# Two attention blocks on one core: the first sum of exponentials, the statistics and the inverted sums are moved

## The chip, the core and the metric

The kernel runs on one core of a Trainium2 chip. The metric is the device time of one launch in microseconds (us), smaller is better. Five engines work side by side, each with its own instruction stream: TensorE (PE; PEld are its weight loads), VectorE (DVE), ScalarE (ACT), GpSimd (POOL) and SyncE (SP), which issues the DMAs here.

## The reference

Eight images of 512 channels and 32 x 32 pixels pass through two layers of the same kind; all is float32.

```python
def layer(x, gn_w, gn_b, wq, bq, wk, bk, wv, bv, wp, bp):   # x: (8, 512, 32, 32)
    xn = group_norm(x, 8 groups, eps=1e-5) * gn_w + gn_b
    q, k, v = (xn @ w.T + b  for w, b in ((wq, bq), (wk, bk), (wv, bv)))   # 1024 tokens, 512 channels
    attn = softmax(q @ k.T * 64 ** -0.5)                    # 8 heads of 64 channels
    return x + (attn @ v) @ wp.T + bp
out = layer(layer(x, layer 0's weights), layer 1's weights)
```

## The kernel before

**Jobs.** A job is one image in one layer: 16 jobs, in the order images 0 and 1 in layer 0, images 0 and 1 in layer 1, images 2 and 3 in layer 0, and so on (`jobs`, L100). The main loop (L941 to L1005) works for step n at the attention of job n and then at the products of job n + 1, while job n + 2's normalisation is being prepared.

**Phases of a step.**
- Attention of job n (`Attention.run`, L724). There are 8 groups, each a pair of heads and a half of the queries, and 8 steps in each group. A step makes scores (`scores`, L641: eight products of 64 x 64 tiles), their exponential on ScalarE (L656), the running sum of the exponentials on VectorE (L660 for the first two, L662 for the rest) and, two steps later, the products with v (`values`, L664). At certain steps a "chore" of the next job is recorded: the statistics of its normalisation (`reads`, steps 4, 8, 12, 16 and 17), its groups' means and its scaling (`steps`, from step 24), and the sums of blocks `t[0]`, `t[1]` (steps 56 and 60).
- The v products of job n + 1 (`v_phase`, L420), the output products of job n (`proj_phase`, L454) and the k and q products of job n + 1 (`deep_phases`, L491).

These products are made by block formulas with seven products instead of eight (`chain`, L377, once for v and output, twice nested for k and q). In a chain the products with numbers 1, 5, 6, 2, 7, 3, 4 are accumulated in four PSUM banks named z, y, u and w. Products 1, 6, 7 and 4 use the same bank, so product 4 waits until the result of product 7 is taken from it (`put`, L540: L549 or L551 on VectorE). In `deep_phases` there are seven chains for k (numbers 0 to 6) and seven for q (7 to 13); two chains are always interleaved, each in its half of the PSUM. After product 7 and after product 3 of a chain one waiting addition of larger blocks (L567, collected in `outer`) is recorded. The last three products of the last q chain are recorded after the first two scores of the attention (L1001 to L1004), so that in this place no other chain stands between products 7 and 4.

**Order.** The orders on TensorE, ScalarE and VectorE are as written in the program; the tile framework adds the waits. `later(delay, fn)` records `fn` when an estimated clock, advanced by hand (`advance`), has gone on by `delay`.

**The end of a group** (`finish`, L681). VectorE reduces the sums over the rows and transposes the result (L688, to `r`). Four DMAs bring `r` to 32 partitions (`lr`, L694). ScalarE copies one half of the values' products from PSUM (L697) and VectorE adds the other half into q's place (L698), which frees the PSUM banks. Some 7.6 us later `invert` (L702) adds the four parts, inverts and transposes them (L706 to L708), sends them to DRAM (`rd`, L709), follows the largest sum and inverse (L710, L711), and two DMAs spread the result over 64 partitions each (`rb`, L713). At 14.6 us `normalise` multiplies (L718). After the last group of a job the delays are 6.0 and 11.5, and `out_sums` (L759) reads the result from 12.6 on.

**Weights.** They come through a ring of eight tiles (`fetch`, L166), each fetched when a tile is released. For the first job of a layer `prepare` (L188) makes the inner weight sums of k and q on VectorE, four operations for each chain. For job 0 the outer weight sums too are made on the way: `factor` (L148) for v0, k0 and q0; q0 stands in the place of image 1's tile.

Of the kernel before, what the change touches and what calls it, by code (L numbers as in the profile page):

```python
# [18 lines left out]
P = 128  # L19
# [51 lines left out]
def fast_path(  # L71
# [20 lines left out]

    out_bias = acts.tile([P, 2, NC], F32, name="out_bias")
    bias_step = acts.tile([P, 2, 2, 2], F32, name="bias_step")
    lmax = acts.tile([RP, RP], F32, name="lmax")
    nc.gpsimd.memset(lmax, 1.0)
    rmax = acts.tile([RP, RP], F32, name="rmax")
    nc.gpsimd.memset(rmax, 1.0)

    jobs = [(b0 + i, layer) for b0 in range(0, B, 2) for layer in range(2) for i in range(2)]  # L100
# [7 lines left out]
    def advance(us):  # L108
        clock[0] += us
        due = [t for t in todo if t[0] <= clock[0]]  # L110
        for t in due:
            todo.remove(t)
            t[1]()
# [101 lines left out]
    class Norm:  # L215


        def __init__(self, n):
            b, layer = jobs[n]
            self.n, self.layer, self.xt = n, layer, xs[b]  # L220
            self.stats = small.tile([P, NC, 2, 6], F32, tag="stats", name=f"stats_{n}")
            self.mv = small.tile([P, NC, 2], F32, tag="mv", name=f"mv_{n}")
            self.mr = small.tile([P, NC, 2], F32, tag="mr", name=f"mr_{n}")
            self.mul = small.tile([P, NC], F32, tag="mul", name=f"mul_{n}", bufs=1)

        def stat(self, cc):
            for sh in range(2):
                nc.vector.bn_stats(
                    self.stats[:, cc, sh, :], self.xt[:, cc, sh * HALF : (sh + 1) * HALF]
                )  # L230
            nc.vector.bn_aggr(
                self.mv[:, cc, :], self.stats[:, cc, :, :].rearrange("p s k -> p (s k)")
            )

        def gather(self):

# [29 lines left out]

        def scale(self, cc, cols=slice(0, S)):
            nc.vector.tensor_scalar(
                xn[0][:, cc, cols], self.xt[:, cc, cols], self.mr[:, cc, 0:1],
                self.mul[:, cc : cc + 1], ALU.subtract, ALU.mult,  # L270
            )

# [29 lines left out]
    def norm_steps(n):  # L302
        norm = Norm(n)

        def scale(cc):
            if cc == 0:
                norm.factors(slice(0, NC))
                xn[0] = acts.tile([P, NC, S], F32, tag="xn", name=f"xn_{n}")
            norm.scale(cc)

        shift = norm.shift
        reads = [lambda cc=cc: norm.stat(cc) for cc in range(NC)] + [norm.gather]
        steps = [norm.groups]
        for cc in range(NC + 1):
            def both(cc=cc):
                if cc > 0:
                    shift(cc - 1)
                if cc < NC:
                    scale(cc)
            steps.append(both)  # L320
        return reads, steps
# [166 lines left out]

        return half_phase(n, O, src, to, group, ORDER)

    def deep_phases(n):  # L491


        layer = jobs[n][1]
        dst = {}
        chains = [(K, o) for o in OUTER] + [(Q, o) for o in OUTER]
# [89 lines left out]
        def thunk(c, j):  # L586
            def go():
                if j == 0:
                    live[c] = begin(c)
                live[c](ORDER[j])  # L590
                if ORDER[j] in (7, 3) and outer:
                    outer.popleft()()
                if j == 6:
                    end(c)
                    if c + 1 == len(chains):
                        while outer:
                            outer.popleft()()
                advance(0.43)

            return go  # L600
# [30 lines left out]
    class Attention:  # L631
# [8 lines left out]

        def scores(self, i):  # L641
            n, q, k = self.n, self.q, self.k
            groups, steps, es, acc = self.groups, self.steps, self.es, self.acc
            g, kc = steps[i]
            hp, sh = groups[g]
            sc = two_banks("sc", f"sc_{n}_{i}")
# [8 lines left out]
            e = epool.tile([P, 2, HALF], F32, tag="e", name=f"e_{n}_{i}")  # L655
            nc.scalar.activation(e, sc, AF.Exp, scale=SCALE)  # L656
            es[i] = e
            if kc == 1:
                acc[g] = apool.tile([P, 2, HALF], F32, tag="acc", name=f"acc_{n}_{g}")
                nc.vector.tensor_add(acc[g], es[i - 1], e)  # L660
            elif kc > 1:
                nc.vector.tensor_add(acc[g], acc[g], e)  # L662

# [15 lines left out]
                    )  # L679

        def finish(self, g):  # L681
            n, q = self.n, self.q
            groups, acc, po = self.groups, self.acc, self.po
            hp, sh = groups[g]
            cols = slice(sh * HALF, (sh + 1) * HALF)
            a = acc.pop(g)
            r = small.tile([P, RP], F32, tag="r", name=f"r_{n}_{g}")
            nc.vector.tensor_reduce(  # L688
                r, a.rearrange("p j (b e) -> p (j b) e", e=RP), AX.X, ALU.add,
                apply_transpose=True,  # L690
            )
            lr = small.tile([RP, NQ, RP], F32, tag="lr", name=f"lr_{n}_{g}")
            for i in range(NQ):
                nc.sync.dma_start(lr[:, i, :], r[i * RP : (i + 1) * RP, :])  # L694
            p = po.pop(g)
            px = apool.tile([P, HALF], F32, tag="px", name=f"px_{n}_{g}")
            nc.scalar.copy(px, p[:, 0, :])  # L697
            nc.vector.tensor_add(q[:, hp, cols], p[:, 1, :], px)  # L698
            rd = dram.tile([2, HALF], F32, tag="rd", name=f"rd_{n}_{g}")
            rb = apool.tile([P, HALF], F32, tag="rb", name=f"rb_{n}_{g}")  # L700

            def invert():  # L702
                lt = small.tile([RP, RP], F32, tag="lt", name=f"lt_{n}_{g}")
                ri = small.tile([RP, RP], F32, tag="ri", name=f"ri_{n}_{g}")
                rt = small.tile([RP, RP], F32, tag="rt", name=f"rt_{n}_{g}")
                nc.vector.tensor_reduce(lt, lr.rearrange("p a b -> p b a"), AX.X, ALU.add)  # L706
                nc.vector.reciprocal(ri, lt)
                nc.vector.transpose(rt, ri)  # L708
                nc.sync.dma_start(rd.rearrange("j (b e) -> (j b) e", e=RP), rt)  # L709
                nc.vector.tensor_max(lmax, lmax, lt)  # L710
                nc.vector.tensor_max(rmax, rmax, ri)  # L711
                for j in range(2):
                    nc.sync.dma_start(  # L713
                        rb[j * HD : (j + 1) * HD, :], rd[j : j + 1, :].to_broadcast([HD, HALF])
                    )

            def normalise():
                nc.vector.tensor_mul(q[:, hp, cols], q[:, hp, cols], rb)  # L718

            ends = g + 1 == len(groups)  # L720
            later(6.0 if ends else 7.6, invert)
            later(11.5 if ends else 14.6, normalise)

        def run(self, chores):  # L724

            steps = self.steps
            for i in range(2, len(steps) + LEAD):
                if i < len(steps):
                    self.scores(i)
                self.values(i - LEAD)  # L730
                g, kc = steps[i - LEAD]
                if kc == NT - 1:
                    self.finish(g)
                    advance(0.85)
                if i in chores:
                    chores[i]()
                advance(1.71)

    def judge():
        nc.vector.tensor_max(lmax, lmax, rmax)  # L740
        worst = small.tile([RP, RP], F32, tag="worst", name="worst")
        nc.vector.tensor_copy(worst, lmax)
        nc.vector.tensor_reduce(worst[:, 0:1], lmax, AX.X, ALU.max)
        turned = small.tile([RP, RP], F32, tag="turned", name="turned")
        nc.vector.transpose(turned, worst)
        top = small.tile([1, 1], F32, tag="top", name="top")
        nc.vector.tensor_reduce(top, turned[0:1, :], AX.X, ALU.max)
# [131 lines left out]
            norm.scale(cc, cols)  # L879
            norm.shift(cc, cols)  # L880

    norm.stat(0)
    norm.stat(1)
    mean, var = norm.means_by_products(0, lambda: idle_products(0, "y", "again_a"))
    mean()
    var()
    for i in range(3):
        idle_products(i % 2, "y", f"again_b{i}")
    norm.stat(2)
    norm.factors(slice(0, 2))  # L890
    normed((0, 1), left)
    normed((0, 1), right_)
    nc.gpsimd.tensor_add(v0[:, S1], v0[:, S3], v0[:, A22])
    norm.stat(3)
    first[0]()
    mean, var = norm.means_by_products(1, lambda: None)
    mean()
# [31 lines left out]

    deep_sums(0, 0.2, 12.0)  # L930
    later(5.0, first_plan)
    for part in range(4):
        later(16.0 + 0.9 * part, lambda part=part: factor(q0, part))
    later(20.0, lambda: store_factors(q0, 0, Q))
    later(21.0, lambda: store_factors(v0, 0, V))
    later(30.0, lambda: load_x(1))
    for thunk in first[6:-1]:
        thunk()
    advance(0.0)
# [1 line left out]
    for n in range(-1, len(jobs)):  # L941
        last = n + 1 == len(jobs)
        if n >= 0:
# [2 lines left out]
                w = plain_weights(n)  # L946
            else:
                t = sums(n + 1)
                chores = dict(zip((4, 8, 12, 16, 17), reads))
                chores.update(zip((24, 36, 40, 44, 48, 52), steps))  # L950
                chores.update({56: t[0], 60: t[1]})
                more = {}
# [29 lines left out]
            for thunk in proj[:-1]:  # L982
                thunk()
            rest = proj[-1:]
        both = deep_phases(n + 1)
        prepare((n + 1, K, OUTER[0]))
        prepare((n + 1, K, OUTER[1]))
        both[0]()
# [1 line left out]
        if n >= 0 and jobs[n][1] == 1 and jobs[n][0] + 2 < B:  # L990
            x_tile(jobs[n][0] + 2)
            load_x(jobs[n][0] + 2)
        reads = steps = []
        if n + 2 < len(jobs):
            reads, steps = norm_steps(n + 2)
        for thunk in both[1:-3]:
            thunk()
        att_n = n + 1
# [256 lines left out]
```

## Time and profile before

| what | value |
|---|---|
| median of three runs | 3313.01 us (3311.23 to 3315.83) |
| profiled execution, its own time | 3314.39 us |
| its span, first to last instruction | 3312.6 us |
| mean granted TensorE clock | 0.995 |
| idle time of VectorE before L660, for ScalarE | 54.7 us in 38 waits |
| idle time of VectorE before L706, for the DMA of lr | 75.7 us in 47 waits |
| idle time of VectorE before L718, for the DMA of rb | 36.9 us in 16 waits |
| L228, one bn_stats of 128 x 512 | 0.68 us, 128 times |
| L231, one bn_aggr | 0.21 us, 64 times |
| L706 to L711, one inversion's five operations | 0.36, 0.34, 0.20, 0.14, 0.17 us, 128 times each |

The profile shows one execution. A line such as `L551 DVE ... p<-vd` is the operation of line 551 on VectorE that writes tile p from tile vd. A wait row names the waiting instruction, an arrow, what ended the wait, and then the total in us, how often and the longest. In a timeline the first number is the start from the span's beginning and the second the duration; in brackets is how long the engine was idle before it, and what ended that. Matmuls are pipelined and their ends are modelled, and a few matmul records are missing.

### The profile page before, as it was taken

What the parts mean: (1) busy time and instruction counts of PE and PEld (TensorE: products, weight loads), DVE (VectorE), ACT (ScalarE), POOL (GpSimd) and SP (SyncE); (2) the same over time, 40 slices, a digit from 0 to 9 for tenths busy, and PEclk for the clock granted to TensorE, in tenths of its full rate; (3) what the DMA queues carried; (4) which work ended last, traced back from release to release, by engine and by line L of the source; (5) the groups of instructions that cost most, each with busy time, mean ns of one, the idle gap of its engine ahead of it and who ended that gap; (6) DMA issues with size and microseconds to landing.
All of it is one profiled execution on the core that took longest, in us unless ns stands there. A gap on an engine that the chain in (4) does not pass through costs nothing.

```text
span 3312.6 us, 56298 instructions
## 1 busy us (share of the span) xinstructions
PE 3257.2 (98%) x22240; PEld 1726.5 (52%) x22240; DVE 2588.3 (78%) x3625; ACT 1729.6 (52%) x2561; POOL 25.2 (1%) x32
## 2 busy tenths in 40 slices
PE   9999999999999999999999999999999999999999
PEld 7356373563735537355473554636556364563643
DVE  8886978879687795877958779596795967869676
ACT  4635636356363664636636365463654636546363
POOL 0000000000000000000000000000000000000000
PEclk9999999999999999999999999999999999999999
DMA  8233151230502204032150221304114031130401
GB/s 297 69 105 99 63 161 61 89 120 22 170 22 72 69 25 120 19 103 89 31 164 18 85 59 38 107 19 137 54 41 154 19 102 39 46 98 21 131 24 44
DMA packets 162399, 265.59 MB, mean 80 GB/s; under 512 B 61144, under 2 KB 72528, under 8 KB 161104
## 3 DMA queue, kind: packets, MB, share of 16 engines
q1 hardware_dynamic: 162128, 261.93, 25.7%
q8 instruction: 176, 2.88, 0.4%
q14 instruction: 95, 0.78, 0.1%
HBM read 214.84 MB, written 44.89 MB: 78 GB/s over the span
## 4 chain that ended last, share of the span: by engine, by line
PE 74%; DVE 17%; issue 4%; DMA 3%; SPq 1%; ACT 1%; DVEq 0%; POOL 0%; ACTq 0%
PE sc L651 17%; PE po L676 16%; DVE acc L662 9%; PE vd L535 8%; PE zd L535 7%; PE z L468 6%; PE z L433 5%; PE yd L535 3%; PE ud L535 3%; DVE acc L660 2%; DMA lr<-r 2%; PE v L468 2%; PE y L468 2%; PE u L468 2%; PE y L433 1%
## 5 line engine op out<-in xcount | busy, mean ns | idle before, releaser
L656 ACT ACTIVATE e<-sc 128x1024 f32<-128x1024 f32 x1024 | 1046.6, 1024 | 596.6 <-PE sc L651 537.8
L651 PE MATMUL sc<-q,k 64*64 64x512 f32 x8192 | 1067.4, 594 | 2.2 <-ACT e L656 2.2
L676 PE MATMUL po<-e,v 64*64 64x512 f32 x8192 | 1061.6, 592 | 0.0
L662 DVE TENSOR_TENSOR acc<-acc,e 128x1024 f32<-128x1024 f32 x768 | 936.1, 1219 | 80.6 <-ACT e L656 31.4
L676 PEld LDWEIGHTS po<-e,v 64*64 64x64 f32 x8192 | 310.9, 134 | 574.9 <-issue 561.7
L651 PEld LDWEIGHTS sc<-q,k 64*64 64x64 f32 x8192 | 307.5, 134 | 570.8 <-issue 547.7
L535 PE MATMUL vd<-deep,w 128*128 128x256 f32 x960 | 271.8, 384 | 31.0 <-DVE p L551 30.3
L535 PE MATMUL zd<-deep,w 128*128 128x256 f32 x832 | 232.4, 379 | 0.5 <-DVE p L551 0.5
L535 PEld LDWEIGHTS vd<-deep,w 128*128 128x128 f32 x960 | 179.7, 190 | 74.3 <-DVE p L551 37.2
L660 DVE TENSOR_TENSOR acc<-e,e 128x1024 f32<-128x1024 f32 x128 | 155.3, 1213 | 54.7 <-ACT e L656 54.7
L535 PEld LDWEIGHTS zd<-deep,w 128*128 128x128 f32 x832 | 157.8, 190 | 29.4 <-issue 6.9
L688 DVE TRANSPOSE_TENSOR_REDUCE r<-acc 128x32 f32<-128x1024 f32 x128 | 158.3, 1237 | 0.5
L384 ACT COPY yd<-vd 128x256 f32<-128x256 f32 x128 | 45.7, 357 | 185.4 <-PE vd L535 178.2
L718 DVE TENSOR_TENSOR q<-q,rb 128x512 f32<-128x512 f32 x128 | 86.0, 672 | 36.9 <-DMA rb<-rd 36.9
L468 PE MATMUL z<-to,w 128*128 128x512 f32 x240 | 110.3, 592 | 0.0
L433 PE MATMUL z<-w,xn 128*128 128x256 f32 x480 | 110.1, 382 | 0.0
L433 PE MATMUL z<-w,t 128*128 128x256 f32 x480 | 108.6, 379 | 0.6 <-DVE v L448 0.6
L468 PE MATMUL z<-q,w 128*128 128x512 f32 x240 | 107.9, 592 | 0.0
L706 DVE TENSOR_REDUCE lt<-lr 32x32 f32<-32x128 f32 x128 | 46.3, 362 | 75.7 <-DMA lr<-r 75.7
L433 PEld LDWEIGHTS z<-w,xn 128*128 128x128 f32 x480 | 90.0, 190 | 23.8 <-issue 12.2
L388 ACT COPY u<-z 128x512 f32<-128x512 f32 x62 | 35.3, 570 | 121.8 <-PE z L468 85.1
L433 PEld LDWEIGHTS z<-w,t 128*128 128x128 f32 x480 | 91.2, 190 | 13.5 <-DVE v L448 1.0
(171 smaller groups left out, 3407.7 us busy)
## 6 DMA issues: line engine op xcount, KB each, us to landing
w<-deep SPq DMA_DIRECT2D x196, 448.0 KB
w<-keep SPq DMA_DIRECT2D x226, 256.0 KB
rb<-rd SPq DMA_DIRECT2D x256, 128.0 KB
out_dram<-x SPq DMA_DIRECT2D x64, 256.0 KB
x<-x_dram SPq DMA_DIRECT2D x28, 512.0 KB
deep<-w SPq DMA_DIRECT2D x28, 448.0 KB
keep<-raw SPq DMA_DIRECT2D x5, 1792.0 KB
lr<-r SPq DMA_DIRECT2D x512, 4.0 KB
```

The lines of the kernel that those rows point to most:

```text
L384: nc.scalar.copy(y, z)
L433: nc.tensor.matmul(ps[:, ti * CH : (ti + 1) * CH], r[:, cc, t0 : t0 + P], w[:, cc, :], start=(start and ti == 0 and cc == 0), stop=(cc == ...
L468: nc.tensor.matmul(ps, w[:, cc, i * P : (i + 1) * P], r[:, cc, :], start=(start and cc == 0), stop=(cc == 1), skip_group_check=True,)
L535: nc.tensor.matmul(ps, lhs[:, FACTOR[i], :], moving[i], start=start, stop=True, skip_group_check=True,)
L651: nc.tensor.matmul(sc[h * HD : (h + 1) * HD, j, :], k[r, hp, k0 : k0 + HD], q[r, hp, sh * HALF : (sh + 1) * HALF], start=True, stop=True,)
L656: nc.scalar.activation(e, sc, AF.Exp, scale=SCALE)
L660: nc.vector.tensor_add(acc[g], es[i - 1], e)
L662: nc.vector.tensor_add(acc[g], acc[g], e)
L676: nc.tensor.matmul(po[g][j * HD : (j + 1) * HD, h, :], v[r, kc, d0 : d0 + HD], e[r, j, :], start=(kc == 0), stop=(kc == NT - 1),)
L688: nc.vector.tensor_reduce(r, a.rearrange("p j (b e) -> p (j b) e", e=RP), AX.X, ALU.add, apply_transpose=True,)
L706: nc.vector.tensor_reduce(lt, lr.rearrange("p a b -> p b a"), AX.X, ALU.add)
L718: nc.vector.tensor_mul(q[:, hp, cols], q[:, hp, cols], rb)
```

## The change

Four things are done.

1. `scores` no longer records the running sum for the first two steps of a job; the first sum (L660) is recorded at the start of `run`, behind the last three q products and the additions of `outer`.
2. The statistics are cut into eight pieces (one bn_stats each, every second with its bn_aggr). From job 2 on, the pieces for job n + 2 and the gathering of the means are recorded among the q products of job n + 1, where `outer` is empty after product 7 or 3 of chain 7 and later, with what is left behind the last product. For job 1 the pieces are chores at steps 2 to 10 of job 0's attention. The q0 factors of job 0 are recorded in the same way, from chain 0 on, and the load of image 1 at 12 us.
3. `finish` makes the sums of two groups, an even and the next odd one, into one tile and inverts them together when the odd one is done: four DMAs to `lr` for two groups, one reduction, one inverse, two transposes, one DMA to `rd`, four to `rb`, and two multiplications, one after the other.
4. The first factor of v0 is made by VectorE, ahead of the statistics of the fourth chunk, and no longer by GpSimd. Some small tiles have one buffer in place of two.

```diff
-        def stat(self, cc):
-            for sh in range(2):
-                nc.vector.bn_stats(
-                    self.stats[:, cc, sh, :], self.xt[:, cc, sh * HALF : (sh + 1) * HALF]
+        def stat(self, cc, sh):
+            nc.vector.bn_stats(
+                self.stats[:, cc, sh, :], xs[self.b][:, cc, sh * HALF : (sh + 1) * HALF]
+            )
+            if sh == 1:
+                nc.vector.bn_aggr(
+                    self.mv[:, cc, :], self.stats[:, cc, :, :].rearrange("p s k -> p (s k)")
                 )
...
-        reads = [lambda cc=cc: norm.stat(cc) for cc in range(NC)] + [norm.gather]
+        reads = [lambda cc=cc, sh=sh: norm.stat(cc, sh) for cc in range(NC) for sh in range(2)]
+        reads.append(norm.gather)
...
-    def deep_phases(n):
+    def deep_phases(n, extra=()):
+        extra = deque(extra)
...
-                if ORDER[j] in (7, 3) and outer:
-                    outer.popleft()()
+                if ORDER[j] in (7, 3):
+                    if outer:
+                        outer.popleft()()
+                    elif extra and extra[0][0] <= c:
+                        extra.popleft()[1]()
                 if j == 6:
                     end(c)
                     if c + 1 == len(chains):
                         while outer:
                             outer.popleft()()
+                        while extra:
+                            extra.popleft()[1]()
...
             es[i] = e
+            if i > 1:
+                self.add(i)
+
+        def add(self, i):
+            g, kc = self.steps[i]
+            acc, e = self.acc, self.es[i]
             if kc == 1:
...
         def finish(self, g):
+            n, q, m = self.n, self.q, g % 2
+            hp, sh = self.groups[g]
+            to_ = q[:, hp, sh * HALF : (sh + 1) * HALF]
+            if m == 0:
+                self.r = small.tile([P, 2, RP], F32, tag="r", name=f"r_{n}_{g}", bufs=1)
+                self.place = []
             nc.vector.tensor_reduce(
-                r, a.rearrange("p j (b e) -> p (j b) e", e=RP), AX.X, ALU.add,
-                apply_transpose=True,
+                self.r[:, m, :], self.acc.pop(g).rearrange("p j (b e) -> p (j b) e", e=RP), AX.X,
+                ALU.add, apply_transpose=True,
             )
...
+            self.place.append(to_)
+            if m == 0:
+                return
+            lr = small.tile([RP, NQ, 2, RP], F32, tag="lr", name=f"lr_{n}_{g}", bufs=1)
+            for i in range(NQ):
+                nc.sync.dma_start(lr[:, i], self.r[i * RP : (i + 1) * RP])
...
-                nc.vector.tensor_reduce(lt, lr.rearrange("p a b -> p b a"), AX.X, ALU.add)
+                nc.vector.tensor_reduce(lt, lr.rearrange("p a g b -> p g b a"), AX.X, ALU.add)
                 nc.vector.reciprocal(ri, lt)
-                nc.vector.transpose(rt, ri)
-                nc.sync.dma_start(rd.rearrange("j (b e) -> (j b) e", e=RP), rt)
+                for i in range(2):
+                    nc.vector.transpose(rt[:, i, :], ri[:, i, :])
+                nc.sync.dma_start(rd.rearrange("m j (b e) -> (j b) m e", e=RP), rt)
...
-                for j in range(2):
-                    nc.sync.dma_start(
-                        rb[j * HD : (j + 1) * HD, :], rd[j : j + 1, :].to_broadcast([HD, HALF])
-                    )
+                for i in range(2):
+                    rb.append(apool.tile([P, HALF], F32, tag="rb", name=f"rb_{n}_{g}_{i}"))
+                    for j in range(2):
+                        nc.sync.dma_start(
+                            rb[i][j * HD : (j + 1) * HD, :],
+                            rd[i, j : j + 1, :].to_broadcast([HD, HALF]),
+                        )
...
-            later(11.5 if ends else 14.6, normalise)
+            later(11.5 if ends else 14.6, lambda: normalise(0))
+            later(12.2 if ends else 16.4, lambda: normalise(1))
...
         def run(self, chores):
             steps = self.steps
+            self.add(1)
...
-    nc.gpsimd.tensor_add(v0[:, S1], v0[:, S3], v0[:, A22])
-    norm.stat(3)
+    factor(v0, 0)
+    for sh in range(2):
+        norm.stat(3, sh)
...
-    for part in range(4):
-        later(16.0 + 0.9 * part, lambda part=part: factor(q0, part))
-    later(20.0, lambda: store_factors(q0, 0, Q))
-    later(30.0, lambda: load_x(1))
...
-                chores = dict(zip((4, 8, 12, 16, 17), reads))
+                chores = dict(zip(range(2, 18), reads)) if n == 0 else {}
...
-        both = deep_phases(n + 1)
+        reads = steps = []
+        if n + 2 < len(jobs):
+            reads, steps = norm_steps(n + 2)
+        if n < 0:
+            extra = [(0, lambda part=part: factor(q0, part)) for part in range(4)]
+            extra.append((1, lambda: store_factors(q0, 0, Q)))
+        else:
+            extra, reads = [(7, fn) for fn in reads], []
+        both = deep_phases(n + 1, extra)
...
+        if n < 0:
+            later(12.0, lambda: load_x(1))
```

## The prediction

> **What bounds the kernel now.** First the page's row of busy times:
>
> ```profile
> PE 3257.2 (98%) x22240; PEld 1726.5 (52%) x22240; DVE 2588.3 (78%) x3625; ACT 1729.6 (52%) x2561; POOL 25.2 (1%) x32
> ```
>
> TensorE sets the end. At most its idle 55 us can go, unless some busy time is slow. So next the waits of TensorE alone (total us, times, longest):
>
> ```profile
> PE vd L535 <- DVE p L551: 30.3, 17, 1.8
> PE v L433 <- DVE q L698: 11.8, 10, 2.6
> PE sc L651 <- ACT e L656: 2.2, 4, 0.9
> PE vd L535 <- DVE p L549: 0.7, 1, 0.7
> ```
>
> The first row is one place, met 16 times (1.79 each), and one wait of 1.64 in job 0. The timeline of job 1 shows it, where the last q chain meets the first scores (start, us, instruction, idle before):
>
> ```profile
> 295.27 0.59 PE L535 MATMUL ud<-t,w 128*128 128x256 f32 x2
> 295.98 1.23 DVE L660 TENSOR_TENSOR acc<-e,e 128x1024 f32<-128x1024 f32 x1 [2.04 <-ACT e L656]
> 297.12 0.48 DVE L551 SCALAR_TENSOR_TENSOR p<-vd,vec_sb,s 128x256 f32<-128x256 f32 x1
> 297.52 1.21 DVE L567 TENSOR_TENSOR q<-q,p 128x1024 f32<-128x1024 f32 x1
> 297.65 0.70 PE L535 MATMUL vd<-deep,w 128*128 128x256 f32 x2 [1.79 <-DVE p L551]
> 298.65 0.48 DVE L551 SCALAR_TENSOR_TENSOR p<-ud,vec_sb,s 128x256 f32<-128x256 f32 x1
> 299.23 1.23 DVE L567 TENSOR_TENSOR q<-p,p 128x1024 f32<-128x1024 f32 x1
> ```
>
> The sum of two exponentials (L660) waits for ScalarE at the head of VectorE's queue. Behind it stands the eviction L551, which frees the bank of the last q product.
>
> Then stretches of 3.41 us around the same place (TensorE, weight loads, VectorE, ScalarE, GpSimd busy, granted clock):
>
> ```profile
> 292.29:295.70 3.41, 3.41 (x23) 1.40 (x22) 1.65 (x3) 2.76 (x5) 0.00 (x0) 1.00 0.27 77
> 295.70:299.11 3.41, 1.62 (x11) 0.66 (x14) 3.13 (x4) 0.72 (x2) 0.00 (x0) 1.00 0.02 5
> 299.11:302.53 3.42, 3.42 (x20) 1.05 (x16) 2.46 (x3) 1.02 (x1) 0.00 (x0) 0.50 0.67 187
> 302.53:305.94 3.41, 3.41 (x36) 1.23 (x32) 1.48 (x2) 2.05 (x2) 0.00 (x0) 1.00 0.85 266
> ```
>
> The stretch after the idle one runs at clock 0.50: 20 matmul records instead of 36, "busy" throughout. So the wait is paid twice. Such a half-clock stretch follows at 206.95, 299.11, 916.93, 1121.73, 2145.73, 2350.53, 2555.33, 2760.13 and 2964.93: eight after this wait and one (206.95) after a wait of 2.58 for L698.
>
> [...] The boundaries are multiples of 3.413 us from 206.95; by them the wait lay wholly inside one window in nine jobs, eight of which were throttled (not the one at 506.69), and where it was cut in two, 1.72 us at most falling in one, none was. [...]
>
> **The change part by part.** In the built program the order on TensorE and ScalarE is unchanged; only VectorE, SyncE and one GpSimd operation move.
>
> 1. First sum behind the last product (16 places). L551's operand is ready when the preceding vd products end (295.43 in the matmul records); VectorE starts 0.02 after a product in other rows. So L551 runs 295.45 to 295.93, and the last product starts at about 295.98 instead of 297.65: 1.67 saved. Next late is the second L551 (ud), again behind an L567 of 1.21, at the same distance as before; values wait for it 0.1, as now. 16 x 1.67 = 26.7 gained.
>
> 2. With no idle of 1.79 left there, the eight half-clock stretches go: each costs half of 3.413, 1.71. 8 x 1.71 = 13.7.
>
> 3. Statistics in pieces. bn_stats is 0.68 (L228), the aggregate 0.21. Jobs 1 to 14 do eight pieces among the q products instead of four pairs at attention steps 4 to 16. The room in the q half, VectorE alone, job 6:
>
> ```profile
> 1310.92 0.42 DVE L549 TENSOR_TENSOR p<-vd,s 128x256 f32<-128x256 f32 x1 [1.67 <-PE vd L535]
> 1311.26 1.22 DVE L567 TENSOR_TENSOR q<-p,p 128x1024 f32<-128x1024 f32 x1
> 1312.39 0.42 DVE L549 TENSOR_TENSOR p<-ud,s 128x256 f32<-128x256 f32 x1
> 1313.94 0.48 DVE L551 SCALAR_TENSOR_TENSOR p<-zd,vec_sb,s 128x256 f32<-128x256 f32 x1 [1.13 <-PE zd L535]
> ```
>
> Each chain leaves about 1.0 to 1.7 idle just where a piece of 0.68 or 0.85 goes. An eviction can also be some 0.74 late before TensorE notices (the 1.64 wait: product at 48.33, so due at 46.69; with the 0.245 wait at 63.95 the due time is 63.71 and the undelayed eviction ends near 62.92). Cost nothing; without that cover, 0.85 a chain. Two pieces fall behind the last product, ahead of the first sum: VectorE starts attention 2 to 3 us behind, makes up 0.5 a step (1.22 of work in 1.72), and five e buffers cover it. Exception: job 2, whose chains also prepare weights (four of 0.28, 1.0 in all); there about 0.2 is left per chain, so lateness builds up: 0.8 lost, bounds 0 and 3. Input x for the first-layer statistics has landed: issued at 672.5, last packet 680.8, first piece after 693. The gather's two DMAs wait on SyncE with nothing urgent behind.
>
> 4. Two groups inverted together. One inversion takes 1.08 from L706 to the next sum (0.36 + 0.34 + 0.20 + 0.14 + 0.17); the pair adds 128 elements to the reduction [...], a second transpose (0.20) and little else: 1.5 for two instead of 2.16. What counts is the end of an attention, where VectorE is behind and L698 holds up the second group of v products (second wait row). The timeline there, job 5:
>
> ```profile
> 1229.83 1.22 DVE L333 TENSOR_TENSOR t<-xn,t 128x1024 f32<-128x1024 f32 x1
> 1230.96 0.35 DVE L706 TENSOR_REDUCE lt<-lr 32x32 f32<-32x128 f32 x1
> ...
> 1232.03 3.86 DVE L662 TENSOR_TENSOR acc<-acc,e 128x1024 f32<-128x1024 f32 x3
> 1235.93 1.25 DVE L688 TRANSPOSE_TENSOR_REDUCE r<-acc 128x32 f32<-128x1024 f32 x1
> 1237.10 0.65 DVE L698 TENSOR_TENSOR q<-po,px 128x512 f32<-128x512 f32 x1
> ```
>
> Group 6's inversion vanishes from here (-1.08), groups 5 and 7 each get a second normalising product (+0.6) and lose an inversion; groups 5 to 7 together give about 1.1. Taking 1.1 off each of the ten waits (2.58, 2.59, 1.53, 0.57, 0.18, 1.14, 1.82, 0.87, 0.21, 0.30) leaves 4.2 of 11.8: 7.6 gained (0 to 11.8). The 2.58 falls to 1.5, so its half-clock stretch goes: 1.7.
>
> Against it: in the v phase VectorE waits for rb already (36.9 us in 16 waits, L718). Now four broadcasts of about 0.54 issue stand behind one rd, and two products follow. I take the second product as ending 1.0 later than today's (bounds 0 and 3), 1.7 later against TensorE, which starts earlier. The evictions L448 behind have 1.5 to 2 of slack, but none in job 2 (TensorE waits 0.55 for L448 at 638.97). So 1.7 in job 2, 0.5 in job 0, 0.8 over the rest: 3.0 lost, bounds 0 and 12. The w fetch that stood between rd and rb now stands behind; its weights are a phase away.
>
> 5. Small parts. factor(v0, 0) moves from GpSimd (1.27) to VectorE ahead of the last statistics: 0.7 on the path at the start (TensorE waits for pm at 15.41). The q0 factors run by slots: two of 0.68 leave the queue ahead of the eviction that TensorE awaits at 48.33, 1.2 gained, 0.2 given back at 63.95. load_x(1) now stands ahead of two q-weight fetches; 2 MB take 7 us and those weights were wanted some 10 us after issue: 0.7 lost, bounds 0 and 3. At the end rb's second pair comes about 1.5 later, just as the second half of the last products needs it: 0.3.
>
> Sum: -26.7 - 13.7 - 7.6 - 1.7 - 1.0 + 0.8 + 3.0 + 0.7 + 0.7 + 0.3 = -45.2. The profiled execution took 3314.39 (span 3312.6), so 3269.2; the median of the runs, 3313.01, is 1.4 below it, so 3268.
>
> **The rivals.**
> - The tail wait is replaced (15%): with two pieces and two L567 ahead, exponential 3 waits for its buffer (the final L567 frees it; I find only 0.2 of room) and TensorE loses 1 us in each job. No half-clock stretch. 3268 + 16 = 3284.
> - The half-clock stretches have another cause than the wait (5%): for it, 506.69; against it, eight of nine. 3268 + 15 = 3283.
> - VectorE at the end of attention gains nothing and the late rb costs 1 us a job more (10%): 3268 + 9 + 14 = 3291.
> - Slower (6%): rb late in the v phase. If the second rb lands 6 us later than today's, L448 holds up the v products in all 15 phases by about 4, long enough to halve the clock in most: 15 x (4 + 1) = 75, 3343. Break-even is 3 us a phase, a landing 5 late. For it: SyncE waits 134.7 us for rd landings (128 times, about 1.05). Against: bytes per phase at this point grow by only 256 KB.
> - The change does not do what it says (2%): a wait still keeps L551 behind the first sum. The built order speaks against it; then 3313.
>
> **How the numbers follow.** The forecast has 62%. Its own bounds: all of L698's wait gone and no loss in the v phase, 3268 - 4 - 3 - 3 = 3258; v phase +9, L698 +8, job 0 and 2 +4 do not all come together: 3280. Range of eight in ten, with the rivals at 3283 to 3291: 3257 to 3293. A measurement can tell about 0.2%, 6.6 us, from no change. Faster 0.92 (62 + 15 + 5 + 10), same 0.02, slower 0.06.
>
> **What would show it.** Waits of TensorE: the row vd behind L551 below 6 us, most single waits below 0.3; v behind L698 near 4; granted clock without 0.50 stretches; L706 64 times at about 0.5. Wrong if a new row of more than 10 us stands there (z behind L448, ScalarE's e behind L567), or if the half-clock stretches stay.

## The result, and the profile after

| | median, us | range | of the kernel before |
|---|---|---|---|
| before | 3313.23 | 3311.23 to 3315.83 | |
| after | 3256.66 | 3255.77 to 3257.97 | 0.9829 (95%: 0.9812 to 0.9846) |

The change takes 56.6 us between the medians and 58.6 between the two profiled executions (3314.39 to 3255.77; spans 3312.6 to 3254.0). The forecast took 45.2. The page's row of busy times after:

```profile
PE 3238.2 (100%) x22240; PEld 1730.1 (53%) x22240; DVE 2569.5 (79%) x3371; ACT 1729.5 (53%) x2561; POOL 14.4 (0%) x31
```

The same 22240 products are busy for 19.0 us less: some 15 of them are, by our estimate from the clock record (nine stretches of 3.413 at 0.50, 1.71 each), the half-clock stretches, in which a product counts as busy for longer (in the prediction's stretches 20 matmul records fill 3.42 us at 0.50, 36 fill 3.41 at 1.00). TensorE's idle time fell from 55.4 to 15.8, the other 39.6 of the 58.6. What is left of it, TensorE's waits after (total, times, longest):

```profile
PE vd L538 <- DVE p L554: 3.9, 17, 0.4
PE zd L538 <- DVE p L552: 2.0, 1, 2.0
PE pm L287 <- DVE mv L231: 1.5, 2, 1.0
PE first_y L862 <- POOL blk L65: 1.5, 1, 1.5
PE zd L538 <- DVE p L554: 0.8, 3, 0.3
PE vd L538 <- DVE p L552: 0.6, 1, 0.6
PE z L434 <- ACT xn L274: 0.6, 1, 0.6
```

The old L551 is now L554: 30.3 us became 3.9. The row "v behind L698" (L710 now; 11.8 us) is not there at all, nor is the scores' row for an exponential (2.2) or the v products' row for L448 (0.6). One row is new: 2.0 for L552, in job 0.

The place of the first sum, again in job 1 (the timeline of all engines after):

```profile
288.22 0.48 DVE L554 SCALAR_TENSOR_TENSOR p<-vd,vec_sb,s 128x256 f32<-128x256 f32 x1 [1.59 <-PE vd L538]
288.62 1.22 DVE L570 TENSOR_TENSOR q<-q,p 128x1024 f32<-128x1024 f32 x1
...
288.76 0.70 PE L538 MATMUL vd<-deep,w 128*128 128x256 f32 x2 [0.21 <-DVE p L554]
...
289.75 0.48 DVE L554 SCALAR_TENSOR_TENSOR p<-ud,vec_sb,s 128x256 f32<-128x256 f32 x1
...
290.15 0.69 DVE L227 BATCH_NORM_STATS2 stats<-x 128x6 f32<-128x512 f32 x1
...
292.72 1.17 DVE L674 TENSOR_TENSOR acc<-e,e 128x1024 f32<-128x1024 f32 x1
```

and two stretches of 3.41 us around it (TensorE, weight loads, VectorE, ScalarE, GpSimd busy, granted clock):

```profile
286.71:290.12 3.41, 3.19 (x22) 1.34 (x18) 1.90 (x3) 2.40 (x3) 0.00 (x0) 1.00 0.17 61
290.12:293.54 3.42, 3.42 (x36) 1.22 (x32) 3.39 (x6) 2.05 (x2) 0.00 (x0) 1.00 0.67 197
```

The eviction now waits for the product alone, the first sum starts 4.5 us behind the eviction (292.72 against 288.22), and the next stretch runs at full clock. No stretch up to the last instruction is below 1.00 (mean granted clock 1.000, for 0.995 before).

The end of an attention, in job 5, which the prediction priced: the first v products before (the reduction that belongs to them, at 1235.93, stands in the prediction), then the timeline of all engines after:

```profile
1232.18 3.72 PE L433 MATMUL z<-w,xn 128*128 128x256 f32 x16
```

```profile
1205.50 3.72 PE L434 MATMUL z<-w,xn 128*128 128x256 f32 x16
...
1206.83 1.25 DVE L703 TRANSPOSE_TENSOR_REDUCE r<-acc 128x32 f32<-128x1024 f32 x1
...
1207.99 0.65 DVE L710 TENSOR_TENSOR q<-po,px 128x512 f32<-128x512 f32 x1
```

The reduction starts 1.33 us after the v products begin; before it was 3.75 (1235.93 against 1232.18). This distance, the lateness of VectorE, is what the rest turns on. Over the 15 phases it was 2.8 to 6.2 before and is 1.2 to 2.7 after. TensorE waits for the bank only where it is above about 3.4 (2.91: no wait; 3.41: the second group of v products 0.01 later than without; 3.75: 0.35 later). Where the lateness may come from is in VectorE's own waits, before and then after:

```profile
DVE lt L706 <- DMA lr<-r: 75.7, 47, 4.1
```

```profile
DVE lt L724 <- DMA lr<-r: 23.3, 24, 3.4
```

VectorE stood 75.7 us before inversions whose input had not come, and sums queue up behind such a wait (in job 8, below, three run back to back for 3.86 us from 1792.89, after the wait and its inversion). Whether this lateness lasts until the attention ends is what the experiments ask. By the inversion's place in its attention 17.3 us fall to the second, 44.3 to the third, 3.3 to the fourth and 10.8 to the last. The third in job 8, in the timeline of before:

```profile
1782.72 0.28 SPq L254 DMA_DIRECT2D dg<-ga  x1
...
1783.86 1.28 SPq L257 DMA_DIRECT2D mr<-dg  x2
...
1785.23 2.46 SPq L694 DMA_DIRECT2D lr<-r  x4
...
1791.81 0.36 DVE L706 TENSOR_REDUCE lt<-lr 32x32 f32<-32x128 f32 x1 [3.40 <-DMA lr<-r]
```

The four `lr` DMAs stand behind the normalisation's `dg` (which waits for GpSimd, 56.1 us in 15 waits over the run) and `mr` (which waits for `dg`, 12.0 in 15), and are issued 1.8 us after `r` is complete (1783.45); VectorE idles 3.40. With pairs this group, the third, has no `lr` of its own, so this meeting does not exist.

### The profile page after: what moved, and what is told of

Its sections match the earlier page's. It is cut to its first block, busy times and chain, and to the rows that moved or that the text cites. A ratio compares the mean times of both kernels' runs of the same rounds, so it can differ in the third digit from the quotient of the medians.

```text
span 3254.0 us, 55636 instructions
## 1 busy us (share of the span) xinstructions
PE 3238.2 (100%) x22240; PEld 1730.1 (53%) x22240; DVE 2569.5 (79%) x3371; ACT 1729.5 (53%) x2561; POOL 14.4 (0%) x31
## 4 chain that ended last, share of the span: by engine, by line
PE 97%; DVE 2%; DMA 0%; issue 0%; ACT 0%; SPq 0%; POOL 0%; DVEq 0%
PE sc L659 27%; PE po L690 27%; PE vd L538 8%; PE zd L538 7%; PE z L434 7%; PE z L469 6%; PE yd L538 3%; PE ud L538 3%; PE u L434 2%; PE v L434 2%; PE y L434 2%; PE y L469 2%; PE u L469 2%; PE v L469 2%; PE pp L628 1%; DVE p L554 0%
## 5 line engine op out<-in xcount | busy, mean ns | idle before, releaser
L447 ACT COPY v<-z 128x512 f32<-128x512 f32 x32 | 18.8, 586 | 146.4 <-PE z L434 136.1
```

## The experiments

Three theories stand in the expectations. A: L698's wait went because the statistics left VectorE's queue in the attention. B: it went because of the paired inversions, by the number of VectorE's operations. C, formed after the first runs: it is not the number, but where `lr` stands on SyncE. Each time stands beside that of the kernel before, measured with it. The expectations count by the steps of the prediction: their part 3, the statistics, is part 2 of the change, and their part 4, the pairs, is part 3.

**The first sum alone: before with part 1.**

```diff
             es[i] = e
+            if i > 1:
+                self.add(i)
+
+        def add(self, i):
...
+            self.add(1)
             for i in range(2, len(steps) + LEAD):
```

> The kernel before with part 1 alone: the first sum behind the last q product. Forecast's mechanism: the wait of 1.79 falls to about 0.2 in 16 places (25 us) and the eight half-clock stretches behind it go (14 us): 3274 us, and TensorE still waits 11.8 us for L698, with one half-clock stretch behind the wait of 2.58. Rival, that the half clock has another cause than the wait: 3288 us, with stretches at 0.50 still there. Rival, that part 1 only shifts the wait to the first values or the exponentials: above 3300 us.

3274.15 (before 3314.97), ratio 0.9875 (0.9859 to 0.9892): 40.8 us, for the 40.4 of steps 1 and 2. The L551 row is 5.1 in 17 (16 times 0.21 and the 1.64); all nine half-clock stretches are gone; `v` behind the addition (L704 here) stays at 12.0, and so do the waits for `lr`:

```profile
PE v L433 <- DVE q L704: 12.0, 8, 2.6
```

```profile
DVE lt L712 <- DMA lr<-r: 76.5, 46, 4.3
```

The ninth stretch was expected to stay and went by luck: the wait of 2.58 for the addition is still there, but a boundary between two windows split it into 1.23 and 1.35.

**The changed kernel with the first sum back in place.**

```diff
-            if i > 1:
-                self.add(i)
+            self.add(i)
...
-            self.add(1)
```

> The changed kernel with part 1 undone: the first sum again in the scores. Forecast's mechanism: 16 waits of about 1.8 us return (25 us), and about half of them are followed by a half-clock stretch (0 to 27 us, by where the windows fall): 3282 to 3309 us. If parts 3 and 4 had taken away that wait by themselves: 3257 us.

3303.83 (before 3314.97), ratio 0.9964 (0.995 to 0.9979): 47 above the changed kernel, within the 3282 to 3309 expected. All 16 waits of 1.79 return (25.2 us more), and twelve half-clock stretches (20.5, at 1.71 each), not eight. One of them, as in the stretches shown before:

```profile
697.89:701.30 3.41, 1.62 (x13) 0.61 (x15) 2.84 (x4) 0.96 (x2) 0.00 (x0) 1.00 0.00 0
701.30:704.71 3.41, 3.41 (x24) 1.07 (x20) 3.38 (x6) 1.07 (x2) 0.00 (x0) 0.51 0.28 77
```

With boundaries at multiples of 3.413 from 701.37, thirteen of the waits lie wholly inside a window, of which twelve are followed by half clock (not the last, which ends at 3158.33), and the three that a boundary splits are not (1.4 at most in one window).

**The wait filled: before, with two idle 128x512 products, which the output does not need, in the gap ahead of the last q product.**

```diff
-        for thunk in both[-3:]:
+        for thunk in both[-3:-1]:
             thunk()
+        for i in range(2):
+            idle_products(1, "y", f"fill_{n}_{i}")
+        both[-1]()
```

> The kernel before with two products of 128 x 512 that nobody reads put on TensorE into each of the 16 waits, between products 3 and 4 of the last q chain; the wait for VectorE is as long as before. If idleness inside a window halves the clock: the eight stretches at 0.50 go and the time falls by 14 us, to 0.996 of before, though not one wait for data is shorter. If the half clock has another cause: the time of before, stretches still there.

3303.67 (before 3317.85), ratio 0.9957 (0.9941 to 0.9974). The place in job 1, in the timeline:

```profile
292.57 2.20 PE L837 MATMUL fill<-blk 128*128 128x512 f32 x4
...
294.00 0.48 DVE L551 SCALAR_TENSOR_TENSOR p<-vd,vec_sb,s 128x256 f32<-128x256 f32 x1
...
294.61 0.62 PE L535 MATMUL vd<-deep,w 128*128 128x256 f32 x2
```

The last product starts no earlier after its eviction, and yet the time is 14.2 us lower; the eight stretches that are gone are worth 8 times 1.71, 13.7. So what the half clock followed here was TensorE's idleness (1.79 us in each place before), not what VectorE does meanwhile. One stretch is left, after a wait of 2.57 for L698 in job 1, which was not filled. The rival "another cause" falls.

**The changed kernel with single inversions (without part 3 of the change).** `finish`, `judge` and the small tiles are those of before.

```diff
+            lr = small.tile([RP, NQ, RP], F32, tag="lr", name=f"lr_{n}_{g}")
+            for i in range(NQ):
+                nc.sync.dma_start(lr[:, i, :], r[i * RP : (i + 1) * RP, :])
...
-            lr = small.tile([RP, NQ, 2, RP], F32, tag="lr", name=f"lr_{n}_{g}", bufs=1)
-            for i in range(NQ):
-                nc.sync.dma_start(lr[:, i], self.r[i * RP : (i + 1) * RP])
```

> The changed kernel with part 4 undone: each group inverted alone, and only the last group's normalising product at the end. Theory A (VectorE's lag is made early in an attention, by the statistics and by inversions that wait for lr while it is late, and is never made good): without the statistics the lag stays small, L698 costs under 1 us in all: 3257 to 3260 us. Theory B (what counts is the work of the inversions near the end, as predicted): L698 costs about 11 us again: 3268 to 3272 us.

3267.48 (before 3314.97), ratio 0.9853 (0.9836 to 0.9869).

```profile
PE v L434 <- DVE q L712: 6.1, 3, 2.6
```

```profile
DVE lt L720 <- DMA lr<-r: 41.8, 34, 3.6
```

A's time is missed by 7 us and more. The median lies 0.5 below B's range, and B's reason fails: the wait halves to 6.1, all in jobs 0 to 2, although every inversion is back. In jobs 3 to 14 A's reason holds: the lateness is 1.7 to 1.9 and TensorE does not wait, though third inversions still wait 18.6 us for `lr` there. Beside the first sum alone, this kernel has the statistics' operations and their DMAs moved together, so it does not tell which of them counts. That led to C.

**The changed kernel with the statistics back in the attention.**

```diff
-                chores = dict(zip(range(2, 18), reads)) if n == 0 else {}
+                chores = {
+                    4 + 4 * c: lambda two=reads[2 * c : 2 * c + 2]: [fn() for fn in two]
+                    for c in range(NC)
+                }
+                chores[17] = reads[8]
...
-            extra, reads = [(7, fn) for fn in reads], []
+            extra = []
```

> The changed kernel with the statistics of part 3 back in the attention (two pieces at steps 4, 8, 12 and 16, the gathering at 17), pairs kept. Theory A: they make VectorE late in the first groups again, some of it lasts to the end: L698 costs 1 to 6 us, 3258 to 3266 us. Theory B: their place does not matter for the end of an attention: 3257 us, L698 0.

3256.04 (before 3314.97), ratio 0.9818 (0.9802 to 0.9835): the changed kernel's time, which B had expected and A had not. No wait for the addition, though VectorE still idles 37.6 at L724. So of the four ways (first sum always in its new place) neither gives 3274.2, the statistics alone 3267.5, the pairs alone 3256.0, both 3256.7. The last three also hold the small parts of the change, about 1 us together (step 5 in the table below). So the pairs bring the whole 18 us; the statistics bring 7 without them and nothing beside them.

**Theory C: the first sum alone, with the normalisation's DMAs moved along SyncE's queue.** Two kernels, no operation of VectorE added or removed: the gather at step 21 and the means at 30 (first diff), or the means alone at 29 (second).

```diff
-                chores = dict(zip((4, 8, 12, 16, 17), reads))
-                chores.update(zip((24, 36, 40, 44, 48, 52), steps))
+                chores = dict(zip((4, 8, 12, 16, 21), reads))
+                chores.update(zip((30, 36, 40, 44, 48, 52), steps))
```

> The kernel with part 1 alone, and the gathering of the means recorded at step 21 in place of 17, the groups' means at step 30 in place of 24: SyncE then issues lr of group 2 ahead of dg and mr (dm and gm still stand ahead of lr of group 1). Not an operation less on VectorE. Theory C (VectorE's lag comes from inversions that wait for lr, and lr is late because it stands on SyncE behind the statistics' own DMAs): VectorE's wait at the third inversion falls from 45 us to under 10, L698's wait from 12 us to about 6 (only jobs 0 to 2, whose weight factors make VectorE late anyway), time 3265 to 3269 us beside 3274 without the shift. Theory B (only the amount of VectorE's work near the end counts): L698's wait stays 12 us, 3274 us.

```diff
-                chores.update(zip((24, 36, 40, 44, 48, 52), steps))
+                chores.update(zip((29, 36, 40, 44, 48, 52), steps))
```

> The kernel with part 1 alone, and one number changed: the groups' means are recorded at step 29 in place of 24, so that lr of group 2 is issued ahead of dg and mr, without the collision with the weight factors of jobs 0 to 2. Theory C: VectorE's wait at the third inversion 45 us to under 8, L698's wait 12 us to about 6, nearly all of it in jobs 0 to 2; 3266 to 3270 us beside 3274. Theory B (amount of work only): L698's wait 12 us, 3274 us.

3283.02 (before 3317.85), ratio 0.9896 (0.988 to 0.9913), and 3278.91 (before 3314.99), 0.9889 (0.9872 to 0.9905): both slower than the first sum alone, where 3265 to 3270 was expected. TensorE in the second of them:

```profile
PE sc L651 <- ACT e L656: 12.7, 3, 5.7
PE v L433 <- DVE q L704: 5.3, 3, 2.1
```

Both rows are in jobs 0 to 2 only. There the fourth inversion now stands behind more of SyncE's queue (job 0, in the timeline):

```profile
143.06 0.28 SPq L254 DMA_DIRECT2D dg<-ga  x1
...
144.20 1.30 SPq L257 DMA_DIRECT2D mr<-dg  x2
...
145.59 0.55 SPq L161 DMA_DIRECT2D keep<-raw  x1
...
155.09 0.35 SPq L177 DMA_DIRECT2D w<-keep  x1
155.49 2.47 SPq L700 DMA_DIRECT2D lr<-r  x4
...
159.18 0.36 DVE L712 TENSOR_REDUCE lt<-lr 32x32 f32<-32x128 f32 x1 [7.34 <-DMA lr<-r]
```

The weights' fetch (L177) waits 8.9 us for the store ahead of it (L161), and `lr` stands behind both; VectorE idles 7.34, an exponential waits 6.2 for a sum to free its buffer, TensorE loses 4.79, and a half-clock stretch follows. In jobs 3 to 14 TensorE's wait for L704 was 5.1 us with the first sum alone and is 0. So C's mechanism showed in these jobs; the total was missed because what else that queue holds in jobs 0 to 2 had been left out.

**The same from job 3 on.**

```diff
-                chores.update(zip((24, 36, 40, 44, 48, 52), steps))
+                chores.update(zip((24 if n < 3 else 29, 36, 40, 44, 48, 52), steps))
```

> The kernel before with the first sum behind the last product, and with the groups' means at attention step 29 in place of 24, but only from job 3 on; not one operation fewer on VectorE than without that second edit. Theory C (the place of lr on SyncE decides): in jobs 3 to 14 no third inversion waits for lr, the reduction of the last group starts 1.7 to 2.9 us after the v products begin, and the 6.5 us by which the second half of the v products is late in those jobs with the first sum alone go: 6.5 us below the kernel with the first sum alone. Jobs 0 to 2 keep their 7.3 us and gain no wait of the scores for an exponential. Theory B (the number of operations decides): the same time as the kernel with the first sum alone.

> The kernel with the first sum alone again, on the chip of the run that moves the means from job 3 on: 3274 within 3, 12 us of waits for L698's addition (L704 there).

3266.52 (3265.11 to 3268.93; before 3316.65), ratio 0.9851 (0.9835 to 0.9868), against 3275.31 (3273.83 to 3278.33) for the first sum alone, ratio 0.988 (0.9863 to 0.9896), measured with it: 8.8 us. TensorE's wait in the first sum alone and then with the edit, and VectorE's with the edit (76.5 above):

```profile
PE v L433 <- DVE q L704: 11.1, 9, 2.6
```

```profile
PE v L433 <- DVE q L704: 6.7, 3, 2.6
```

```profile
DVE lt L712 <- DMA lr<-r: 39.2, 37, 3.5
```

One number in the program, no operation fewer (3625 on VectorE, as before), and the wait for the addition is left in jobs 0 to 2 alone; in jobs 3 to 14 the last reduction starts 1.7 to 2.6 us into the v phase. Third inversions there wait 0.7 us in all, for 36 before the edit. B falls as the whole cause, and C stands for these jobs as a way that is enough by itself; moving the statistics away was another. In jobs 0 to 2, which hold 6.7 of the 11.8 us, only pairs removed the wait; how much of that is fewer operations and how much fewer `lr` was not separated.

**The meeting put back into the changed kernel: the means at step 32 from job 3 on, ahead of the second pair's `lr`.**

```diff
-                chores.update(zip((24, 36, 40, 44, 48, 52), steps))
+                chores.update(
+                    zip((24, 36, 40, 44, 48, 52) if n < 3 else (32, 39, 43, 47, 51, 54), steps)
+                )
```

> The changed kernel with the collision put back in jobs 3 to 14: the groups' means at step 32 (scaling and the rest later by 2 to 7 steps), so that dg and mr stand on SyncE ahead of lr of groups 2 and 3. Theory C: the second pair's inversion waits for lr, 2 to 4 us in each of these jobs, VectorE's lag at the last group rises from about 1.1 to 2.5 us or more, and TensorE waits for L698 or nearly: 3257 to 3268 us. Theory B: no wait at the second pair, lag as in the changed kernel, 3257 us.

3257.06 (before 3314.99), ratio 0.9819 (0.9803 to 0.9835): no change, at the lower end of C's range and at B's time.

```profile
DVE lt L724 <- DMA lr<-r: 43.4, 34, 3.4
```

The second pair's inversion does wait, as C said and B did not (22.7 us in all, for 1.7), and the lateness in these jobs is 1.5 to 3.2 for 1.2 to 1.6, but it stays below what TensorE notices. So with pairs there is room for one such wait, which single inversions did not have: fewer operations count too, beside the place of `lr`.

**Two more edits to the changed kernel: the second scores between products 3 and 4 of the last q chain, and the load of image 1 later.**

```diff
-            later(12.0, lambda: load_x(1))
+            later(20.0, lambda: load_x(1))
...
-        att.scores(1)
-        for thunk in both[-3:]:
+        for thunk in both[-3:-1]:
             thunk()
+        att.scores(1)
+        both[-1]()
```

> The changed kernel with two edits that should beat it: the second scores stand between products 3 and 4 of the last q chain, so that TensorE has 0.86 us of work while the eviction runs (16 waits of 0.21 go, 3.4 us), and image 1 is loaded at 20 us in place of 12, behind the q weights (the wait of 1.97 us in job 0 goes): 5 us less than the changed kernel. If product 4 or the values then wait for the later exponential instead: no gain, 0 to 5 us more.

> The changed kernel itself, on the chip of these runs, to hold the others against: 0.983 of before.

3252.35 (3251.58 to 3252.51; before 3317.85), ratio 0.98 (0.9786 to 0.9814), beside 3257.82 (3255.09 to 3259.36) for the changed kernel measured with it, ratio 0.9818 (0.9804 to 0.9832): 5.5 us, and no execution of the one is as fast as the slowest of the other. TensorE's waits for k and q evictions in it:

```profile
PE zd L538 <- DVE p L554: 0.8, 3, 0.3
PE vd L538 <- DVE p L552: 0.7, 1, 0.7
PE vd L538 <- DVE p L554: 0.4, 1, 0.4
```

The sixteen waits of 0.21 (3.4 us) and the one for L552 in job 0 are gone. Here that second wait was 1.1 in the profiled execution of the changed kernel, and the two profiled executions are 2.7 apart (3255.09 and 3252.35), so how the 5.5 of the medians divides between the two edits is not shown.

## Why the prediction was right or wrong

In the order of its sum; "measured" is the difference between the two profiled executions.

| term | forecast | measured |
|---|---|---|
| 1. sixteen tail waits | -26.7 | -25.3 (1.79 to 0.21 each) |
| 2. eight half-clock stretches | -13.7 | -13.7 (8 to 0, at 1.71 each) |
| 4. wait for L698 | -7.6 | -13.7 |
| 4. ninth half-clock stretch | -1.7 | -1.7 |
| 4. late rb in the v phase | +3.0 | -0.6 |
| 3. pieces in job 2 | +0.8 | +0.6 (from job 2's v products to job 3's; 0.3 of it in waits) |
| 5. start, pm | +0.7 | +0.1 |
| 5. q0 factors | -1.0 | -1.2 |
| 5. load of image 1 | +0.7 | +2.0 |
| 5. end | +0.3 | -0.9 (last product to end 5.97 to 5.02; no wait of TensorE) |
| not in the sum: scores for an exponential | | -2.2 |
| sum | -45.2 | -56.6, of 58.6; 2.0 are not placed |

- **Steps 1 and 2 were right**, cause and size, and are shown alone (40.8) and from the other side (the filled wait, and the first sum put back). That the stretches were eight is luck of the profiled execution (see the last section).
- **Step 4 failed**, in both of its uncertain terms. The prediction took VectorE's lateness at the end of an attention for the sum of the operations near it: "groups 5 to 7 together give about 1.1". In jobs 3 to 14 the lateness was carried over from inversions earlier in the attention, where VectorE stood idle for `lr`: with the means moved from job 3 on, and no operation fewer, it fell from between 3.1 and 5.4 us to between 1.7 and 2.6. This idleness, 75.7 us in the table of the profile before, was never followed to what it makes late. In jobs 0 to 2 the cause stays open; there, too, pairs gave more than 1.1. The last reduction came 1.6 to 4.2 earlier against the v products, and all the waits went. It was not that the pair's own work shrank more than forecast: a pair takes 1.66 where the prediction held 1.5, its author's estimate; its reduction takes 0.58 for a single one's 0.36, its reciprocal 0.54 for 0.34. Nor are the waits the whole price: the second half of the v products is due 5.28 us after the phase begins, and counted so L698 cost 13.7 before, not the 11.8 of the wait row.
- The same error set **the loss in the v phase**. The second multiplication for rb was to end 1.0 later than before, 1.7 later against TensorE; it starts 1.2 earlier against the v products (15.1 on average, for 16.3). The way to it from the last reduction did get longer, by 1.5, but that reduction comes 2.7 earlier on average. No phase waits for the v values now, and the 0.55 of job 2 went too.
- **The range's lower end rested on this step too**: it allowed "all of L698's wait gone and no loss in the v phase" at its 11.8, which gives 3258. That is what happened; what L698 cost beyond the 11.8, and the scores' 2.2, which the sum held for nothing, came on top. That the end, too, came 0.9 shorter is not shown to be the change: from the last product to the end it was 5.0 to 5.6 over the traces with pairs and 5.2 to 6.0 over those without.
- **Step 3** had the sign right and the reason for its cover: pieces among the q products cost TensorE nothing but in job 2. But their gain was not foreseen: with single inversions the kernel is 7 us faster when the statistics are moved.
- **Step 5**, the load of image 1: 2.0 for 0.7. VectorE's wait in job 0 of the changed kernel, and TensorE's behind it:

```profile
DVE w L151 <- DMA w<-keep: 2.4, 1, 2.4
```

```profile
67.68 0.70 PE L538 MATMUL zd<-deep,w 128*128 128x256 f32 x2 [1.97 <-DVE p L552]
```

The eviction L552 (at 67.21) stands behind weight sums (L151, at 66.27) whose weights come behind the 2 MB of the image: its loads are issued from 55.49 on, the next fetches (`w<-keep`) from 57.63. The prediction had asked when the weights are wanted by TensorE; VectorE wants them earlier. The 2.0 is one execution's: in the other five profiles with this load at 12 us the wait was 1.1 to 3.0, and in three of them (2.1, 2.7, 3.0) a half-clock stretch followed; here a boundary between windows split it into 0.30 and 1.66, and none did. With the load later, as above, it is gone.

Of the rivals, "VectorE gains nothing" and "rb late" had the sign of step 4 the wrong way round, and no buffer of an exponential was missed in the tail: the scores' waits went.

## What to carry to other kernels

When an engine reaches a hand-over late, don't count only the operations just ahead of it; go back to where it last stood idle for something, and ask what that input stood behind in the queue of the engine that issues it. A tiny DMA that a busy engine will wait for should not be recorded behind one that itself waits for another engine; moving one number along the queue was worth nearly as much in most jobs here as inverting in pairs (from the v products of job 3 to those of job 15: 2428.4 us with the first sum alone, 2420.7 with the means moved, 2418.9 with pairs). And before a move along a shared queue is priced, look at that queue in the unusual jobs too.

## What the runs showed of the hardware

- The clock was halved after TensorE had been idle for only a part of a window of 3.413 us: 1.79 us of it in the stretches of job 1 before (295.70 to 299.11, then 3.41 us at 0.50). The boundaries between windows, which each trace's own clock record gives (before: every half-clock stretch starts a multiple of 3.413 us after 206.95), split some waits; of each wait the longest piece inside one window is taken. Over all fourteen traces, in windows at full clock: each of the 13 pieces of 2.00 to 3.41 us was followed by a stretch at 0.50; of the 22 waits of 1.79 or 1.80 at the end of the q products that lay wholly inside a window 20 were (where one was split and left 1.73, no stretch followed); of six pieces of 1.72 to 1.99 in the v products none was; nor was any of 1.71 or less. So the length of the idle piece alone does not decide between 1.7 and 2.0; what else does is open, and so is why the waits at 506.69 (before) and 3158.33 (the first sum put back) were spared.
- The windows make a fixed loss depend on the length of a job. With the first sum put back a late job takes 204.85 us, 60 windows are 204.80, so the wait moves along the window by only 0.05 a job and, once inside, stayed there for thirteen jobs. Of two kernels with the same sixteen waits one paid eight half-clock stretches for them and the other twelve: 7 us that no operation explains. Executions of one kernel differ in the same way: of eight of the kernel before, the fastest (3312.19) had a mean granted clock of 0.995 and the slowest (3323.83) 0.992, by our estimate from these clocks some ten and some sixteen stretches, which is most of the 11.6 us between them.
